# Three bf16 passes in place of f32 products: the scores and relative terms of the last of four layers

## The chip, the cores and the metric

The kernel runs on 1 core of one Trainium2 chip. The metric is the device time of one execution in microseconds (us). Several executions are timed; one more is taken with the hardware profiler, and everything read from a trace belongs to that one.

The engines are TensorE (PE; its weight loads are shown apart as PEld), VectorE (DVE), ScalarE (ACT), GpSimd (POOL) and SyncE (SP). SP issues nearly all DMA transfers here.

## The reference, cut to what matters

The network takes x of 4 sequences by 1024 tokens by 128 features through four layers. Each layer normalizes x, computes an attention-like branch `s` and a feed-forward branch `g`, and adds `s * silu(ffn)`. The change touches the fourth layer, a causal attention of 16 heads of 8 features with a relative term:

```
xn  = layernorm(x)
q, k, v = split_heads(xn @ Wq.T), split_heads(xn @ Wk.T), split_heads(xn @ Wv.T)     # (b, 16, n, 8)
ex  = rel_embed[ns].reshape(n, 16, 8).transpose(1, 0, 2)                             # 256 embeddings
srel = srel_skew(einsum('bhnd,hmd->bhnm', q, ex))      # row n shifted so that column = distance
qk  = (einsum('bhnd,bhmd->bhnm', q, k) + srel) / sqrt(8)
att = softmax(qk - 1e9 * triu(1, k=1))                 # causal
s   = einsum('bhnm,bhmd->bhnd', att, v) @ Wp.T + bp
g   = silu(gated feed-forward of xn, hidden size 384)
out = x + s * g
```

All inputs and outputs are float32, except the integer weights of this layer's feed-forward.

## The kernel before, in words

Layers 0 to 2 come first and hold x in SBUF (`x_all`). Layer 2 writes x to DRAM (`x3`). Then `load3` and `prepare3` load and turn the weights of the last layer, and `layer3` does the rest. An instruction stream for each engine is recorded while the Python code runs; the engines follow their streams in order and meet through semaphores. The order on one engine is close to that of the code, but a scheduler moves some instructions.

**The embeddings.** `prepare3` spreads the 256 embeddings with POOL copies into a zeroed tile `pad` (L1653), turns it on PE and has `W["emb"]`: 8 features of one head on partitions 32j to 32j+7, for j = 0 to 3, and 256 distances in columns. The column of distance 0 is subtracted from the others (L1660, L1661). Distances beyond 255 need no relative term then.

**A batch begins.** `begin3` loads one sequence of x, normalizes it, turns it (`xnT`), multiplies by `WqT` and `WkT` in two halves of 512 tokens (L1835), copies the products by ACT into `qk` (L1836), and stores them in DRAM (L1837). Values go the same way (`v`, `vd`). For the first sequence all of it runs at once, before the loop. For the others it is a generator (`beside`) that the loop moves on by one step a unit, from the fourth unit of the third group of the sequence before.

**Groups, units and tiles.** A group is 4 heads of one sequence; there are 16. `project3` loads the group's q and k from DRAM into `q` and `kk`, head j on partitions 32j to 32j+7. A group has 8 units, one for each block of 128 queries, in the order `ORDER3 = (7, 0, 6, 1, 5, 2, 4, 3)`, so that long and short rows take turns. A unit with t+1 blocks of keys has one tile of up to 512 columns, or two where t is over 3: 192 tiles in all.

**The relative term.** `relative3` multiplies 128 queries by the 256 embeddings, for two heads and two blocks at a time (L1914, in row slots 32j of PE's array), copies the result by ACT into `r` (L1916) and stores it in DRAM as `flat` with rows of 384 (L1919, L1920). `shear3` reads it back with a row step of 383 (L1935, L1937, L1941), which turns the column into the distance to the query, as the tile `rel`. POOL then sets what lies before or behind with affine selects (L1945). The tile of long units (`relb`) is in the pool `p2` with two buffers, that of short ones (`rels`) in `p1` with one. The loop calls `part(n + 7)` for `relative3` and `ahead(n + 3)` for `shear3`.

**Scores.** `scores3` multiplies q by k for 4 heads side by side (L1978, row slots 32j, one PSUM bank for each head, one set of 4 banks). DVE adds rel, scales, and keeps the running minimum `low` (L1993; L1986 for columns that need no rel). ACT takes the exponential and the row sums (L2000). DVE turns 32 by 32 blocks (L1737) and PE weighs the values (`weigh3`, L2014), in pieces that the loop puts between tiles. `vb` is the tile of values, filled by POOL (`values3`, L1899) when the last unit of the group before has been weighed; `drain(values)` stands in `weigh`.

**The loop.** It goes over the tiles:

```
next(fill, None)                      # DVE's comparison of this tile
transpose(...)                        # of an older tile, on DVE
step()                                # a piece of weighing, on PE
next(fill, None)                      # the score products of the next tile, on PE
```

At the last tile of a unit there follow the next group's `project3`, `part(n + 7)`, `values3`, a step of `beside`, and `ahead(n + 3)`.

`temp` is a pool of three buffers of 4 KB a partition, shared by x, the normalized x, `qk`, `v`, `r` and tiles of the feed-forward.

Of the kernel before, what the change touches and what calls it, by code (L numbers as in the profile page):

```python
# [19 lines left out]
P = 128  # L20
# [9 lines left out]
def _constants():  # L30
# [7 lines left out]

    parts.append(("ident", np.eye(P)))
    parts.append(("tri", row <= col))  # L40
# [5 lines left out]

    parts.append(("sel3", (row // 32 == col // 8 % 4) & (row // 8 % 4 == col // 32)))
    parts.append(("of_a", (row // 8 % 4) == np.arange(4)[None, :]))
    parts.append(("of_t", (row % 8) == np.arange(8)[None, :]))
# [43 lines left out]
class Kit:  # L93


    def __init__(self, tc, const, const_sb):
        self.tc, self.nc = tc, tc.nc
        self.const_sb = const_sb
# [6 lines left out]
    def c(self, name):  # L105
        at, n = CONST_AT[name]
        return self.const_sb[:, at : at + n]
# [1511 lines left out]
def spread(a):  # L1619

    return a.rearrange("p (i j r) -> p i j r", j=4, r=32)[:, :, :, 0:8]
# [6 lines left out]
def prepare3(k, w, W, ps):  # L1628
# [18 lines left out]
    W["emb"] = new("emb", [P, 4, 256])  # L1647
    with k.tc.tile_pool(name="pad3", bufs=1) as rp:
        pad = rp.tile([P, 2, 512], F32, tag="pad", name="pad")
        nc.vector.memset(pad, 0.0)  # L1650
        for c in range(2):
            for i in range(4):
                nc.gpsimd.tensor_copy(spread(pad[:, c, :])[:, i], heads_of(W["rel"][:, c, :])[:, i])  # L1653
        for i in range(4):
            k.transpose_tiles(ps, "tr", [pad[:, c, i * P : (i + 1) * P] for c in (0, 1)], W["emb"][:, i, :])

        e0 = rp.tile([P, 4], F32, tag="e0", name="e0")
        nc.vector.tensor_copy(e0, W["emb"][:, :, 0])
        for i in range(4):
            nc.vector.tensor_scalar(W["emb"][:, i, :], W["emb"][:, i, :], e0[:, i : i + 1], None, op0=ALU.subtract)  # L1660
        nc.vector.tensor_scalar(W["emb"][:, :, 0], e0, -1.0, None, op0=ALU.mult)  # L1661
# [10 lines left out]
def layer3(k, W, x3, out, eps5, ps):  # L1672
# [12 lines left out]
    with ExitStack() as st:  # L1685
# [16 lines left out]
        def ahead(n):  # L1702
            if n < len(units):
                t = units[n][2]
                rels[n] = shear3(k, p2 if t > 3 else p1, flats[n // 8, t // 2], t)
# [5 lines left out]
        batch[0] = {}  # L1711
# [9 lines left out]
        weights, transposes, weighs, out_of = {}, [], [], {}  # L1721
# [19 lines left out]
        def weigh(n):  # L1741
            nonlocal values
            b, i, t = units[n]
            at, pair = n // 8, t // 2
            if n % 8 == 2:
                out_of[at] = ps.tile([P, 8, 32], F32, tag="o", name="po")
            o = out_of[at]
            yield from weigh3(k, weights.pop((at, pair)), vb, o, pair)
            if n % 8 == 7:
                drain(values)  # L1750
# [18 lines left out]
        for x, (n, first) in enumerate(tiles + [(len(units), 0)] * 4):  # L1769
# [16 lines left out]
            if pos == 3 and i == 2 and b + 1 < NB:  # L1786
                batch[b + 1] = {}
# [7 lines left out]
            if pos == 6 and at + 1 < 4 * NB:  # L1795
                values = values3(k, p1, batch[(at + 1) // 4], vb, (at + 1) % 4)
                next(values)
            next(beside, None)
            ahead(n + 3)
# [13 lines left out]
def begin3(k, W, p1, p2, temp, ps, dram, x3, b, eps5, seq):  # L1813
# [4 lines left out]
    k.layernorm(p2, x.rearrange("p h a d -> p (h a) d"), xn, eps5)  # L1818
# [10 lines left out]
    seq["qk"] = dram.tile([2, P, T], F32, tag="qk", name="qk")  # L1829
    for n, name in enumerate(("WqT", "WkT")):  # L1830
# [314 lines left out]
```

## Time and profile before

| | |
|---|---|
| median of 3 runs | 3271.13 us (3264.41 to 3277.84) |
| the profiled execution's own time | 3261.59 us |
| its span, first to last instruction | 3259.9 us |
| mean granted TensorE clock in it | 0.734 |
| DVE's first comparison of the last layer | 2208.69 us from the span's start |
| busy from there to 3238.4 us: PE, DVE, ACT, POOL | 865, 807, 626, 290 of 1029.7 us |

Lines such as L1978 are lines of the kernel before. In a group of instructions, `out<-in` names the tiles; then come partitions x elements, the count, busy time in us and the mean duration of one in ns, and after the second bar the time that the engine had been idle just before, with what ended it. In a row of windows, the first number after the bounds is the length, then the busy time of each engine with the count of instructions, then the granted share of the TensorE clock, the busy share of the 16 DMA engines and GB/s. In a timeline the columns are start, duration and engine. A wait line has the waiting group, what it waited for, us in total, times, and the longest.

### The profile page before, as it was taken

Reading aid. Unit: us, or ns where it says so; the run is one execution under the profiler, and the core shown is the slowest. Engines: PE = TensorE matmul, PEld = TensorE weight load, DVE = VectorE, ACT = ScalarE, POOL = GpSimd, SP = SyncE. Lnnn points to the kernel's source line nnn. Section 1 sums busy time; section 2 is a strip of 40 time slices with the busy share of each in tenths; the row PEclk is TensorE's granted clock in tenths of the full one; section 3 lists DMA queues with packets and bytes.
Section 4 is the critical chain, followed back from the end, with each engine's and each line's share of the span. In section 5 each row is a group of like instructions: output and inputs, shape, how many; then the busy total and the mean of one; then the engine's idle time right before and its main releaser. Section 6 shows DMA issues by size and latency. Waiting matters only on the chain. (4 is left out here: it accounts for less than half of the span.)

```text
span 3259.9 us, 50636 instructions
## 1 busy us (share of the span) xinstructions
PE 2317.2 (71%) x18321; PEld 1327.2 (41%) x18321; DVE 2307.1 (71%) x5534; ACT 1487.5 (46%) x3248; POOL 1174.5 (36%) x1104
## 2 busy tenths in 40 slices
PE   5787777677776777965533772557888888888885
PEld 2555555222322323651101222344545555555553
DVE  5555545878878886657868878437678778777786
ACT  4555453433333334344322561125665665755663
POOL 3344334144444444224577222332322322323322
PEclk9888888678788888985555666566766766756676
DMA  3000000100000000320433444347677677766772
GB/s 89 3 1 1 1 1 1 35 0 0 0 0 1 0 0 33 105 84 0 111 95 105 109 108 99 110 119 209 187 213 207 181 209 217 202 195 193 200 231 71
DMA packets 396446, 303.46 MB, mean 93 GB/s; under 512 B 96272, under 2 KB 380812, under 8 KB 390564
## 3 DMA queue, kind: packets, MB, share of 16 engines
q1 hardware_dynamic: 395044, 296.03, 32.2%
q10 hardware_dynamic: 1152, 4.19, 0.4%
q8 instruction: 144, 2.36, 0.3%
q14 instruction: 106, 0.87, 0.1%
HBM read 160.63 MB, written 138.94 MB: 92 GB/s over the span
## 5 line engine op out<-in xcount | busy, mean ns | idle before, releaser
L2000 ACT ACTIVATE neg<-neg,low 128x640 f32<-128x640 f32 (+7 forms) x512 | 390.0, 763 | 153.9 <-DVE low L1993 153.8
L1945 POOL TENSOR_SCALAR_AFFINE_SELECT rel<-rel 128x512 f32<-128x512 f32 x288 | 179.9, 637 | 565.6 <-DMA rel<-flat 357.3
L1737 DVE STREAM_TRANSPOSE wT<-neg 128x640 f32<-128x640 f32 (+7 forms) x512 | 362.0, 753 | 7.6 <-ACT neg L2000 6.9
L1978 PE MATMUL score<-k,q 8*128 8x512 f32 (+3 forms) x1536 | 295.0, 747 | 91.2 <-DVE low L1993 91.0
L1993 DVE CUSTOM_DVE_ANT_0 neg<-score,rel,low 128x128 f32<-128x128 f32 (+3 forms) x448 | 217.5, 516 | 152.5 <-PE score L1978 105.6
L1914 PE MATMUL pr<-emb,q 8*128 8x256 f32 x1024 | 245.2, 569 | 45.0 <-ACT r L1916 27.2
L2014 PEld LDWEIGHTS po<-wT,vb 128*32 128x32 f32 x10240 | 208.1, 140 | 143.3 <-issue 78.0
L2014 PE MATMUL po<-wT,vb 128*32 128x64 f32 (+1 forms) x10240 | 242.9, 259 | 31.7 <-issue 17.3
L1914 PEld LDWEIGHTS pr<-emb,q 8*128 8x128 f32 x1024 | 153.6, 269 | 124.4 <-ACT r L1916 62.9
L1916 ACT COPY r<-pr 128x512 f32<-128x512 f32 x256 | 138.4, 581 | 144.2 <-PE pr L1914 95.1
L1993 DVE CUSTOM_DVE_ANT_0 neg<-score,rel 128x512 f32<-128x512 f32 (+3 forms) x320 | 149.3, 520 | 26.7 <-issue 15.4
L1978 PEld LDWEIGHTS score<-k,q 8*128 8x128 f32 x1536 | 103.0, 249 | 153.9 <-DVE low L1993 127.8
L835 PE MATMUL pg<-xnT,w 128*128 128x512 f32 x256 | 148.4, 663 | 7.7 <-DVE h L839 4.5
L214 PE MATMUL pt<-ident,three 128*24 128x128 bf16 x64 | 9.2, 295 | 201.9 <-DVE three L211 201.9
L788 POOL TENSOR_TENSOR prod<-rest,kv 128x2048 f32<-128x2048 f32 x32 | 145.6, 4599 | 18.4 <-ACT rest L778 18.4
L837 PE MATMUL pu<-xin,w 128*128 128x512 f32 x256 | 140.5, 632 | 14.3 <-DVE h L839 7.9
L826 PE MATMUL po<-h,w 128*128 128x512 f32 x256 | 129.6, 627 | 27.1 <-DVE h L839 27.1
L838 ACT ACTIVATE h<-pg 128x512 f32<-128x512 f32 x128 | 75.9, 595 | 156.2 <-PE pg L835 152.7
L1986 DVE TENSOR_SCALAR_CACHE_REDUCE neg<-score 128x384 f32<-128x384 f32 (+2 forms) x192 | 79.7, 415 | 69.3 <-PE score L1978 69.3
L1050 PE MATMUL ph<-xin,upT 128*128 128x512 bf16 (+1 forms) x128 | 71.3, 588 | 78.5 <-DVE xin L1044 77.7
L1455 PE MATMUL read<-kt,const_sb 128*128 128x128 f32 x256 | 50.1, 366 | 94.2 <-POOL kt L1450 94.2
L431 PE MATMUL px<-hT,xbcT 128*128 128x512 f32 x256 | 115.4, 595 | 0.0
(621 smaller groups left out, 5690.5 us busy)
## 6 DMA issues: line engine op xcount, KB each, us to landing
flat<-r SPq DMA_DIRECT2D x256, 256.0 KB
rel<-flat SPq DMA_DIRECT2D x112, 512.0 KB
flat<-r SPq DMA_DIRECT2D x256, 128.0 KB
rel<-flat SPq DMA_DIRECT2D x96, 256.0 KB
kt<-kd SPq DMA_DIRECT2D x16, 512.0 KB
qt<-qd SPq DMA_DIRECT2D x16, 512.0 KB
kdc<-kdd SPq DMA_DIRECT2D x16, 512.0 KB
ktc<-ktd SPq DMA_DIRECT2D x16, 512.0 KB
```

What stands on the lines that cost most here:

```text
L788: nc.gpsimd.tensor_tensor(prod, attn.rearrange("p (t h g) -> p t h g", t=4, g=16)[:, t].unsqueeze(2).to_broadcast(each), kv[:, t, 1, :].re ...
L826: nc.tensor.matmul(po, W["w2"][:, e, c, :], h[:, c, :], start=(e == 0 and c == 0), stop=(e == 7 and c == 1))
L835: nc.tensor.matmul(pg, W["w1"][:, e, c * P : (c + 1) * P], xnT, start=True, stop=True)
L837: nc.tensor.matmul(pu, W["w3"][:, e, c * P : (c + 1) * P], xin, start=True, stop=True)
L1737: nc.vector.transpose(weights[at, pair][j][:, t % 2, 0 : (t + 1) * P], S[j][:, 0 : (t + 1) * P])
L1914: nc.tensor.matmul(to[:, m, :], q[at, t * P : (t + 1) * P], W["emb"][at, i, :], start=True, stop=True)
L1916: nc.scalar.copy(r[:, n], to)
L1945: nc.gpsimd.affine_select(out=rel[:, :, slot(back), :], in_=rel[:, :, slot(0), :], compare_op=op, fill=fill, base=0, pattern=[[0, 4], [-si ...
L1978: nc.tensor.matmul(sc[:, j, 0 : last - first], q[at(j), 1 + t * P : 1 + n], kk[at(j), first:last], start=True, stop=True)
L1993: nc.vector.tensor_tensor_reduce(out=neg[:, begin:last], in0=sc[:, j, begin - first : last - first], in1=rel[:, j, slot : slot + (last - b ...
L2000: nc.scalar.activation(neg[:, 0:n], neg[:, 0:n], AF.Exp, bias=here, scale=-1.0, accum_out=group["sums"][:, j, t : t + 1])
L2014: nc.tensor.matmul(o[32 * j : 32 * j + 32, 2 * pair + m.start : 2 * pair + 2, :], vb[:, kb, j].rearrange("p a d -> p (a d)"), weights[j][: ...
```

## The change

The last layer's q, k and embeddings are split into three bf16 parts whose sum is the float32 value: the upper 16 bits, the upper 16 bits of what is left, and the rest. In `begin3`, ACT copies each half of the product to `rest`; POOL copies the upper half-words of `rest` (a bf16 view of it) to `three`, subtracts, and does so again. For each half, q goes to DRAM once with its three parts and k three times, so that 24 rows (8 features by 3 parts of q) meet 24 rows that all hold one part of k. The scores then take three accumulating bf16 matmuls (parts of k), and so do the relative terms (parts of the embeddings). The slots keep their places, 32j, with 24 rows instead of 8. The two q tiles are allocated once and hold two zero columns ahead. `prepare3` copies the embeddings three times into `pad` and splits them with three ACT copies and two DVE subtractions.

All rel tiles come from `p2`. `ahead(n + 3)` and the filling of `vb` now stand ahead of the step of `beside`, and the filling after `ahead`. The constants are loaded in two parts, of which the larger lies in memory that is freed before the last layer. The layernorm's small tiles of `begin3` lie in `p1`.

```diff
 def spread(a):
-    return a.rearrange("p (i j r) -> p i j r", j=4, r=32)[:, :, :, 0:8]
+    return a.rearrange("p (i j r) -> p i j r", j=4, r=32)[:, :, :, 0:24].rearrange("p i j (d a) -> p i j d a", a=3)
...
-                nc.gpsimd.tensor_copy(spread(pad[:, c, :])[:, i], heads_of(W["rel"][:, c, :])[:, i])
+                for a in range(3):
+                    nc.gpsimd.tensor_copy(spread(pad[:, c, :])[:, i, :, :, a], heads_of(W["rel"][:, c, :])[:, i])
...
+        for third in range(3):
+            nc.scalar.copy(W["emb"][:, third], emb)
+            if third < 2:
+                nc.vector.tensor_tensor(emb, emb, W["emb"][:, third], ALU.subtract)
...
-                rels[n] = shear3(k, p2 if t > 3 else p1, flats[n // 8, t // 2], t)
+                rels[n] = shear3(k, p2, flats[n // 8, t // 2], t)
...
             if n % 8 == 7:
-                drain(values)
+                ripe.append(values)
...
+            ahead(n + 3)
+            fill_values()
             next(beside, None)
-            ahead(n + 3)
...
-    seq["qk"] = dram.tile([2, P, T], F32, tag="qk", name="qk")
-    for n, name in enumerate(("WqT", "WkT")):
-        qk = temp.tile([P, T], F32, tag="temp", name="qk")
+    seq["q"] = dram.tile([P, 3, T], BF16, tag="qd", name="qd")
+    seq["k"] = dram.tile([P, 3, 3, T], BF16, tag="kd", name="kd")
+    for name in ("WqT", "WkT"):
         for half in range(2):
             tok = slice(half * 512, (half + 1) * 512)
             pp = ps.tile([P, 512], F32, tag="tr", name="pp")
             nc.tensor.matmul(pp, W[name], xnT[:, tok], start=True, stop=True)
-            nc.scalar.copy(qk[:, tok], pp)
-        nc.sync.dma_start(out=seq["qk"][n], in_=qk)
-        yield
+            three = temp.tile([P, 3, 512], BF16, tag="temp", name="three")
+            rest = temp.tile([P, 512], F32, tag="temp", name="rest")
+            nc.scalar.copy(rest, pp)
+            upper = rest.bitcast(BF16).rearrange("p (t two) -> p t two", two=2)[:, :, 1]
+            for third in range(2):
+                nc.gpsimd.tensor_copy(three[:, third], upper)
+                nc.gpsimd.tensor_tensor(three[:, 2] if third else rest, rest, three[:, third], ALU.subtract)
+            if name == "WqT":
+                nc.sync.dma_start(out=seq["q"][:, :, tok], in_=three)
+            else:
+                for a in range(3):
+                    nc.sync.dma_start(out=seq["k"][:, a, :, tok], in_=three)
+            yield
...
-            at, t = slice(32 * j, 32 * j + 8), 2 * pair + m
-            nc.tensor.matmul(to[:, m, :], q[at, t * P : (t + 1) * P], W["emb"][at, i, :], start=True, stop=True)
+        for third in range(3):
+            for j, to in zip(js, pr):
+                at = slice(32 * j, 32 * j + 24)
+                nc.tensor.matmul(
+                    to[:, m, :], q[at, first : first + P], W["emb"][at, third, i, :], start=(third == 0), stop=(third == 2)
+                )
...
-        for j in range(4):
-            nc.tensor.matmul(
-                sc[:, j, 0 : last - first], q[at(j), 1 + t * P : 1 + n], kk[at(j), first:last], start=True, stop=True
-            )
+        for third in range(3):
+            for j in range(4):
+                nc.tensor.matmul(
+                    sc[:, j, 0 : last - first], q[at(j), 2 + t * P : 2 + n], kk[at(j), third, first:last],
+                    start=(third == 0), stop=(third == 2),
+                )
```

`project3` loads, for each of the four heads, 24 rows of 1024 for q and 24 rows of 3 x 1024 for k, by as many transfers as before. The rest of the diff moves constants.

## The prediction

> **What bounds the kernel now.** First the page: its totals and the row of the granted clock, because the change touches TensorE (PE), GpSimd (POOL) and the DMA queue of SyncE (SP) at once. All edits but one split load lie in the last layer, which starts at 2150 us; the fourth fence cuts it into opening, loop and tail.
>
> ```profile
> span 3259.9 us, 50636 instructions
> PE 2317.2 (71%) x18321; PEld 1327.2 (41%) x18321; DVE 2307.1 (71%) x5534; ACT 1487.5 (46%) x3248; POOL 1174.5 (36%) x1104
> PEclk9888888678788888985555666566766766756676
> ```
>
> Then the groups, for the lines that change:
>
> ```profile
> L1945 POOL TENSOR_SCALAR_AFFINE_SELECT rel<-rel 128x512 f32<-128x512 f32 x288 | 179.9, 637 | 565.6 <-DMA rel<-flat 357.3
> L1978 PE MATMUL score<-k,q 8*128 8x512 f32 (+3 forms) x1536 | 295.0, 747 | 91.2 <-DVE low L1993 91.0
> L1914 PE MATMUL pr<-emb,q 8*128 8x256 f32 x1024 | 245.2, 569 | 45.0 <-ACT r L1916 27.2
> ```
>
> Each f32 matmul stands there as two instructions; scores and relative terms hold 540 us of PE. What that is worth is read from the waits of VectorE (DVE) in the loop (columns: us in total, times, longest):
>
> ```profile
> DVE neg L1993 <- PE score L1978: 105.7, 53, 9.7
> DVE neg L1986 <- PE score L1978: 44.1, 14, 7.3
> ```
>
> ```profile
> 2150.00:2208.70 58.70, 36.30 (x145) 25.29 (x143) 14.01 (x54) 19.86 (x39) 16.50 (x24) 0.65 0.62 174
> 2208.70:3238.40 1029.70, 864.99 (x13166) 544.15 (x13167) 806.94 (x2551) 625.71 (x1474) 289.75 (x414) 0.68 0.68 196
> 3238.40:3259.90 21.50, 9.47 (x140) 5.02 (x140) 2.61 (x6) 0.37 (x1) 4.68 (x2) 0.79 0.09 25
> ```
>
> Columns are length, then busy PE, weight loads, DVE, ACT, POOL, then clock, DMA share and GB/s. In the loop DVE idles 1029.7 - 806.9 = 223 us. I went through the timeline for all 192 groups of scores. In 81 of them DVE stands idle for over 0.3 us (192 us in all) until the last score matmul ends. Between the end of DVE's comparison before and the end of the score those 81 hold 240 us of PE: 125 scores, 22 relative terms, 50 feed-forward, 22 weighting, the rest small, 13 idle. The other 111 groups have their scores ready: a faster PE gives nothing there. So 540 us of faster matmuls cannot return more than these stalls, and a stall shrinks by no more than its own length.
>
> **Three passes for f32.** Two widths of a score group at half clock:
>
> ```profile
> 2653.13 0.81 PE L1978 MATMUL score<-k,q 8*128 8x128 f32 x8
> 2655.34 2.09 PE L1978 MATMUL score<-k,q 8*128 8x512 f32 x8
> ```
>
> (2.09 - 0.81)/384 is 3.33 ns a column and 0.38 us is fixed. No row has four bf16 matmuls beside one another on 32-row slots. Alone, a 24-row bf16 pass of 512 columns (pb, L222) takes 580 ns at the median, a 128-column one (L214) 314: 0.69 ns a column. A quarter of the f32 rate would be 0.83. So three passes of 512 cost 1.06 to 1.28 us plus 0.38, which is 0.69 to 0.79 of 2.09; the weight loads, 98 ns in bf16 (L222) against 281 in f32, shorten the fixed part. I take 0.74 for both kinds. Relative slices begin at an odd column of q, for which no row exists; a bf16 load twice as long would still be shorter than today's. In the 81 stalls, each capped by its length: -37 us (bounds -30 and -43).
>
> **The clock.** The clock records change only at steps of 3.41 us. I sorted the loop's steps by PE time of anything but scores and relative terms: with none, the next step had the full clock in 0 of 84; with 1 to 1.5 us in 24%; with 2 to 3 us in 79%; over 3 us in all 32. In 77 steps of the span the 8-row matmuls were over 90% of PE's work and over 2 us long: the next was at half clock in all 77. The windows say it too; the first is full of 8-row matmuls, the second of weighting (128 rows):
>
> ```profile
> 2192.00:2196.00 4.00, 4.00 (x21) 2.83 (x16) 0.57 (x2) 2.22 (x4) 0.00 (x0) 0.50 1.11 369
> 2240.00:2244.00 4.00, 3.50 (x185) 2.97 (x178) 2.26 (x13) 0.04 (x1) 1.28 (x2) 0.93 1.11 357
> ```
>
> So occupied rows seem to count, and 24 rows are three times 8. With pass lengths at 3/4, work by rows times columns of these two lines rises by 2.25. Recounting each step so, with the limit that parts full from half today (0.35 of the array's full work in a step), full steps go from 36% to 42%, or 0.68 to 0.71 in the mean: 5% faster, another -9 us in the 81 stalls. Below, 24 rows count as little as 8 (0 us). Above, everything runs at full clock: scores and relative terms at 0.50 of today, the rest at 0.65, which leaves -91 us of the stalls in place of -46.
>
> The Trainium skill (TensorE: Matmul & The Clock Gate, Part 1) says that the clock is set by how busy PE has recently been, and that idleness lowers it. The first window above, fully busy at 0.50, does not agree if busy means time. By that rule this change, which leaves PE idler, would cool the clock, and the sum would go towards the fourth rival's.
>
> **Distances with two buffers.** SP's queue waits 226.9 us for DVE's `low` ahead of rel loads (L1935), since the small rel tile has one buffer; flat stores, project and value loads stand behind it. With two, that wait goes; ACT's r (146.7 us at L1919) is late next. DVE waited for rel only at the start, so the worth is bounded by the 13 us in which PE idled inside stalls: 0 to -13, I take -8. The value copies now stand behind the selects on POOL. They are needed two units later, so 0; uncovered, 4 x 1.03 us (L1899) would hold weighting, and the scores behind it in PE's order, in each of 15 groups.
>
> **What the thirds cost at the opening.** Up to the first comparison at 2208.69 nothing covers them.
>
> ```profile
> 2176.84 2.06 SPq L1837 DMA_DIRECT2D qk<-qk  x2
> 2183.57 3.06 SPq L1895 DMA_DIRECT2D vr<-vd  x4
> 2186.90 0.62 SPq L1919 DMA_DIRECT2D flat<-r  x1
> ```
>
> The embeddings first: 24 pad copies instead of 8 (16 x 0.207 = 3.3 us), then two rounds of a 1024-wide ACT copy (1.06, from L778) and a DVE subtraction (1.24, from L2050's 0.69 for 512), 4.6 us. In the order of instructions both subtractions stand before the layernorm, which began at 2165.8 as DVE came free: +7 (5 to 8). Then q and k: per half two POOL copies (0.52, half of L1899's 1024) and two subtractions (1.06, L1127), 3.2 us; four halves from 2175.5 end at 2188.3. SP now stands in the order 2 q stores, 6 k stores, v, 4 q loads, 4 k loads, 4 v loads, then flats. The six stores and v's issue add 2 us after the last half, the k loads wait some 3 us for 1.2 MB at the 300 to 430 GB/s seen then, and 8 issues take 4.4 us: first flat at 2198 to 2199 instead of 2186.9, +12. Dearest rows (0.30 per 128 columns, L1646; 1.92, L1359) make four halves 25 us: +24. Cheapest: +8. From the first flat to the first comparison are 28 stores of 0.55 us on SP, as before. Opening: +19 (13 to 32).
>
> At three batch changes the same POOL work (12.8 us) and 6 more SP issues lie beside 60 us of loop per group. But q's second half is made on the last unit of a group, and the first relative matmuls on it stand three tiles (3 x 1030/192 = 16 us) later in PE's order. ACT's copy 0.6, POOL 3.2, a unit's selects before it 1.9, store 2.8 (2176.84 to 2179.63 above) and load 3.5 are 12 us. I take +5 in sum for the three. Nothing there can gain. Above, each stops PE as long as the longest select waited for rel in the loop (13.8 us, DMA): +41. Traffic grows by 4.2 MB a batch, 16.8 MB in all, 58 us at the loop's 196/0.68 GB/s, in engines that are 68% busy over 1030 us: off the path.
>
> **Sum.** -37 - 9 - 8 + 19 + 5 = -30 us. The profiled execution took 3261.59 us, its span 3259.9; it becomes 3232. The median of the three runs is 9.5 us above it, so I forecast 3241.
>
> **Rivals.**
> 1. The clock wakes: 24 rows count fully. Scores become ready early, DVE and exponentials rule. -91 - 8 + 24 = -75: 3196. For it: 128-row windows at 0.93. Against: bf16 chains of layer 2 ran at 0.5. 18%.
> 2. The stalls change owner: passes give -37 alone, nothing else, against 24: -13, 3258, no measurable change (0.5% is 16 us, about what a measurement of this kernel can tell from none). For it: 50 of 240 us are feed-forward. 21%.
> 3. Slower: q's chain through POOL stops PE at each batch change. 41 there and 28 at the opening, against -37: +32, 3303. It decides from stops of (37 + 9 + 8 - 19)/3, about 12 us each. For it: POOL's selects wait up to 13.8 us for DMA, and the thirds stand behind them. Against: 16 us of slack. 18%.
> 4. The clock sinks to 0.5: 1.36 times all, passes at 1.02: the stalls grow by 33, +57 with the costs, 3328. Against: the 77 steps, in which this work already counts for nothing. 5%.
>
> **Numbers.** My forecast has 38%. Faster by over 0.5% (under 3255): 38 + 18 = 56%; within: 21%; slower: 18 + 5 = 23%. From 3185, just under rival 1, to 3300, just short of rival 3, leaves out about two in ten.
>
> **What would show it.** Score groups of 12 bf16 instructions near 1.55 us at half clock; DVE's waits for scores some 100 instead of 150 us in the loop; clock 0.70 to 0.73 there; first comparison near 2228; SP's wait for `low` gone. I am wrong if the loop's DVE idle time stays near 223 us, if relative matmuls wait for q's DMA by more than 10 us at batch changes, or if the loop's clock leaves 0.66 to 0.76.

## The result, and the profile after

The changed kernel takes 3292.72 us (median; 3284.12 to 3301.32), the kernel before 3262.98 us beside it (eight runs each; the three ahead of the prediction had a median of 3271.13): a ratio of 1.0092, 95% interval 1.0073 to 1.0112. It is slower by some 30 us where 30 us less was forecast. The profiled execution took 3290.7 us, 29 us more than that of before. A ratio is made against the kernel before on the same chip; below, differences between kernels are differences of ratios times 3263 us.

The page after, totals and granted clock:

```profile
span 3288.8 us, 53223 instructions
PE 2189.1 (67%) x19599; PEld 1246.2 (38%) x19601; DVE 2300.4 (70%) x5536; ACT 1488.3 (45%) x3251; POOL 1231.0 (37%) x1170
PEclk9898888688778878975556675656766767777677
```

TensorE lost 128 us of work and the span grew. The groups that answer to those of before (busy us, mean ns, then the idle time before them):

```profile
L1982 POOL TENSOR_SCALAR_AFFINE_SELECT rel<-rel 128x512 f32<-128x512 f32 x288 | 180.3, 637 | 463.3 <-DMA rel<-flat 382.2
L2016 PE MATMUL score<-k,q 24*128 24x512 bf16 (+3 forms) x2304 | 201.8, 431 | 155.1 <-DVE low L2032 150.9
L1949 PE MATMUL pr<-emb,q 24*128 24x256 bf16 x1536 | 196.1, 358 | 77.8 <-ACT r L1953 41.5
```

Scores and relative terms together fell from 540 to 398 us. But idle time before relative matmuls rose from 45.0 to 77.8 us. The last layer again in opening, loop and tail (columns as before):

```profile
2150.00:2233.00 83.00, 33.64 (x175) 20.31 (x175) 15.77 (x56) 22.62 (x42) 32.08 (x52) 0.58 0.55 154
2233.00:3267.70 1034.70, 739.05 (x14407) 467.28 (x14407) 796.51 (x2551) 624.27 (x1474) 329.45 (x448) 0.70 0.76 209
3267.70:3288.80 21.10, 9.30 (x141) 4.97 (x140) 2.57 (x6) 0.37 (x1) 4.68 (x2) 0.80 0.13 26
```

The opening is 24 us longer. The loop has 126 us less PE work, a clock of 0.70 as forecast, and is 5 us longer: DVE idles 238 instead of 223 us in it. The DMA engines go from 68% to 76% busy. What DVE waits for in the loop (us, times, longest):

```profile
DVE neg L2032 <- issue: 113.4, 52, 9.7
DVE neg L2032 <- POOL rel L1982: 85.6, 10, 18.8
...
DVE neg L2032 <- DMA rel<-flat: 11.7, 6, 3.3
DVE neg L2032 <- PE score L2016: 8.3, 10, 3.3
...
DVE neg L2025 <- PE score L2016: 5.1, 4, 2.1
```

In the kernel before, "issue" and the selects stood at:

```profile
DVE neg L1993 <- issue: 42.5, 18, 6.8
DVE neg L1993 <- POOL rel L1945: 13.9, 1, 13.9
```

By this view scores, 150 us before, are nearly gone, POOL's selects stand at 85.6 (13.9 before), and "issue" at 113.4 (42.5), a wait for which the view names nobody. A view that names one releaser per wait misleads here, so I took the score and select times from the trace, group by group: in nearly every stall, before and after, the tile's first comparison starts less than 0.25 us after the last score product ends. Idle time in which the score products ended last is 220 us in 94 groups (215 in 100 before; the prediction, which counted more narrowly, had 192 in 81), and only 13 us are left to selects. In the stalls, from the end of DVE's comparison before to the end of the score products, PE spent:

| us | score | relative | weighing | feed-forward | rest | PE idle | all |
|---|---|---|---|---|---|---|---|
| before | 143 | 27 | 23 | 52 | 12 | 15 | 273 |
| after | 84 | 32 | 18 | 55 | 20 | 49 | 258 |

So the faster passes gave 59 us there, and PE's own waiting took 34 back. Of its 49 us, 21 end at a relative matmul (0.4 before), 12 at a weighing, 7 at a feed-forward product. The stretches are 15 us shorter in sum, but DVE idles for 233 of the 258 us, where it idled for 215 of 273: it has less other work in them.

### The profile page after: what moved, and what is told of

Read it like the earlier page. It is cut to its first block, busy times and chain, and to the rows that moved or that the text cites. A ratio compares the mean times of both kernels' runs of the same rounds, so it can differ in the third digit from the quotient of the medians.

```text
span 3288.8 us, 53223 instructions
## 1 busy us (share of the span) xinstructions
PE 2189.1 (67%) x19599; PEld 1246.2 (38%) x19601; DVE 2300.4 (70%) x5536; ACT 1488.3 (45%) x3251; POOL 1231.0 (37%) x1170
## 5 line engine op out<-in xcount | busy, mean ns | idle before, releaser
L2016 PE MATMUL score<-k,q 24*128 24x512 bf16 (+3 forms) x2304 | 201.8, 431 | 155.1 <-DVE low L2032 150.9
L2053 PE MATMUL po<-wT,vb 128*32 128x64 f32 (+1 forms) x10240 | 231.0, 245 | 58.7 <-issue 37.1
L1949 PE MATMUL pr<-emb,q 24*128 24x256 bf16 x1536 | 196.1, 358 | 77.8 <-ACT r L1953 41.5
L2053 PEld LDWEIGHTS po<-wT,vb 128*32 128x32 f32 x10240 | 193.0, 130 | 139.4 <-issue 69.8
L1949 PEld LDWEIGHTS <-q 24*128 24x128 bf16 x1536 | 114.1, 118 | 152.7 <-issue 91.3
L2016 PEld LDWEIGHTS <-q 24*128 24x128 bf16 x2304 | 71.7, 107 | 227.3 <-issue 182.6
L1457 PE MATMUL read<-kt,last_sb 128*128 128x128 f32 x256 | 49.4, 363 | 94.3 <-POOL kt L1452 94.3
```

The source lines that it names most:

```text
L1949: nc.tensor.matmul(to[:, m, :], q[at, first : first + P], W["emb"][at, third, i, :], start=(third == 0), stop=(third == 2))
L2016: nc.tensor.matmul(sc[:, j, 0 : last - first], q[at(j), 2 + t * P : 2 + n], kk[at(j), third, first:last], start=(third == 0), stop=(third ...
L2053: nc.tensor.matmul(o[32 * j : 32 * j + 32, 2 * pair + m.start : 2 * pair + 2, :], vb[:, kb, j].rearrange("p a d -> p (a d)"), weights[j][: ...
```

## The experiments

All medians and ratios in one table; each kernel is told of below it. The last column is the ratio times 3263 us. A quotient of the two medians can differ from the ratio on record by a few us; it does most in e5, where it gives -15 instead of -21.

| | us | ratio to before, 95% | to before, us |
|---|---|---|---|
| e1 moved steps, f32 | 3283.5 | 1.0054 (1.0035 to 1.0072) | +18 |
| e8 second buffer only, f32 | 3274.3 | 1.0039 (1.0022 to 1.0056) | +13 |
| e2 thirds, old order | 3290.1 | 1.0076 (1.0054 to 1.0097) | +25 |
| e7 next sequence's step first | 3279.5 | 1.0058 (1.0035 to 1.0081) | +19 |
| e3 no thirds on GpSimd | 3263.5 | 0.9994 (0.9983 to 1.0006) | -2 |
| e4 k stored once | 3282.4 | 1.0046 (1.0026 to 1.0065) | +15 |
| e6 narrow second and third pass | 3300.8 | 1.0109 (1.0075 to 1.0143) | +36 |
| e5 one part of k loaded | 3245.9 | 0.9936 (0.9915 to 0.9956) | -21 |
| e9 the same and 393 KB for nobody | 3269.1 | 1.0031 (1.0014 to 1.0047) | +10 |
| e13 e2 with one part of k | 3243.5 | 0.9934 (0.9913 to 0.9955) | -22 |
| e14 f32 and 393 KB for nobody | 3297.8 | 1.0102 (1.0081 to 1.0123) | +33 |
| e10 k loads on ACT's queue | 3280.8 | 1.0072 (1.0046 to 1.0097) | +23 |
| e11 e10, k once, DVE at the opening | 3273.9 | 1.0054 (1.0036 to 1.0072) | +18 |
| e12 e11, q loads on ACT's queue too | 3290.2 | 1.0086 (1.0057 to 1.0116) | +28 |
| e15 old order, k once, k loads spread | 3275.1 | 1.0029 (1.0013 to 1.0046) | +9 |
| e16 e7, k once, DVE at the opening | 3274.7 | 1.0039 (1.0022 to 1.0055) | +13 |
| e17 e15 with six of nine products | 3354.9 | 1.0272 (1.0249 to 1.0296) | +89 |
| e18 e16 with six of nine products | 3284.3 | 1.0060 (1.0039 to 1.0080) | +20 |

**The moved steps and the second buffer.** e1 is the kernel before with all of the change except the thirds.

```diff
-                rels[n] = shear3(k, p2 if t > 3 else p1, flats[n // 8, t // 2], t)
+                rels[n] = shear3(k, p2, flats[n // 8, t // 2], t)
-                drain(values)
+                ripe.append(values)
+            ahead(n + 3)
+            fill_values()
             next(beside, None)
-            ahead(n + 3)
```

> The kernel before with only the moved steps, the second buffer for the small rel tiles and the split constants; products stay f32. Theory A (the loss comes from the thirds of q and k at the opening and at the three batch changes): this kernel has none of them, so it lies at 0 to -13 us from the kernel before, ratio 0.996 to 1.000. Rival B (the loss comes from the moved steps: selects that wait for a load now stand ahead of the feed-forward's products and of the value copies in POOL's queue): it holds most of the loss, +15 to +30 us, ratio 1.005 to 1.009.

e2 is the changed kernel with those lines as they were before.

> The changed kernel with its moved steps undone: small rel tiles with one buffer, ahead(n + 3) after the step of beside, values filled where the last weighing of a group ends. The thirds and the three passes stay. Theory A: the loss stays, 3285 to 3300 us against 3263 of the kernel before (ratio 1.007 to 1.012). Rival B: the passes' gain shows, -37 - 9 + 24 for the opening, so 3235 to 3260 (ratio 0.992 to 0.999).

e8 has only the first pair of those lines, in the kernel before (with the constants in two parts and the layernorm's small tiles in `p1`, which the memory needs).

> The kernel before with the second buffer for the small rel tiles alone (and the split constants): f32 products, old order of the steps. By the prediction's term -8, with 0 to -13 as its bounds: 3253 to 3266 (ratio 0.996 to 1.000). Rival (SP, freed of its wait for low, issues flats and rel loads earlier and these collide with others; the loss of the moved steps comes from the buffer): slower, 3272 to 3284 (ratio 1.002 to 1.006).

e7 is the changed kernel with the step of the next sequence first.

```diff
+            next(beside, None)
             ahead(n + 3)
             fill_values()
-            next(beside, None)
```

> The changed kernel with the step of beside ahead of ahead(n + 3) again, as before; the fill of the values stays where the change puts it, and the small rel tiles keep two buffers. Theory B2 (the selects that stand between the feed-forward's products on GpSimd cost the loop): 8 to 20 us less than the changed kernel, 3273 to 3285 (ratio 1.002 to 1.006). Rival (the scheduler orders GpSimd's queue by what is ready, so that the place in the code does little when rel loads are late): 3288 to 3297 (ratio 1.007 to 1.010).

In f32 the moved steps cost 18 us, and 13 of them come with the second buffer alone; by the forecast it saved 8. No run has the split constants and the layernorm's tiles by themselves; e8's first comparison with rel comes at 2207.75 us, so nothing is lost ahead of the loop. What can be seen in the loop is that the scheduler puts selects between the products `h` of the feed-forward. POOL in e8, first feed-forward step of the second sequence (start, us, engine):

```profile
2533.93 0.73 POOL L1874 TENSOR_TENSOR h<-h,up 128x256 f32<-128x256 f32 x1 [4.96 <-DMA rel<-flat]
2535.45 1.22 POOL L1952 TENSOR_SCALAR_AFFINE_SELECT rel<-rel 128x512 f32<-128x512 f32 x2 [0.79 <-DMA rel<-flat]
2536.63 0.72 POOL L1874 TENSOR_TENSOR h<-h,up 128x256 f32<-128x256 f32 x1
2537.31 0.63 POOL L1952 TENSOR_SCALAR_AFFINE_SELECT rel<-rel 128x512 f32<-128x512 f32 x1
2537.91 0.73 POOL L1874 TENSOR_TENSOR h<-h,up 128x256 f32<-128x256 f32 x1
```

PE of e8 beside it:

```profile
2537.41 0.49 PE L1878 MATMUL po<-downT,h 128*128 128x128 f32 x2 [1.03 <-POOL h L1874]
2538.70 2.08 PE L1878 MATMUL po<-downT,h 128*128 128x128 f32 x8 [0.80 <-POOL h L1874]
```

And POOL of the kernel before at the same step:

```profile
2536.12 2.10 POOL L1867 TENSOR_TENSOR h<-h,up 128x256 f32<-128x256 f32 x3 [2.19 <-ACT up L1866]
2538.16 1.94 POOL L1945 TENSOR_SCALAR_AFFINE_SELECT rel<-rel 128x512 f32<-128x512 f32 x3
```

Before, three products run in one go and the selects after them. In e8 the first product starts when ACT's `up` is done, at 2533.85 (the view puts this wait down to rel). The second could start at 2534.40 by its `up`, but starts 2.2 us later, behind two selects, which waited 0.79 us for their rel transfer; the third stands behind one more select. PE's `po` waits for the products, with the scores behind it. Over the 16 feed-forward steps 13 selects stand among the products in e1 and e8, 1 before, 18 after; DVE's idle time in the feed-forward groups (1, 5, 9, 13) is 97 us in e8 and 86 before. That is 11 of the 22 us that DVE idles longer in the loop of e8's trace; where the rest comes from is open. The count of such selects is no price by itself: the changed kernel has 18 and idles 89 us in these groups, e12 below has none and idles 106. With the thirds, taking the moved steps and the buffer out (e2) gains only 5 us, within the intervals. Their cost does not add to that of the rest. The order in e7 gains 11 us (here the intervals just overlap).

**What the thirds cost on GpSimd.** In e3, ACT writes the bf16 product three times and POOL does nothing, so scores are those of rounded values.

```diff
-            nc.scalar.copy(rest, pp)
...
-                nc.gpsimd.tensor_copy(three[:, third], upper)
-                nc.gpsimd.tensor_tensor(three[:, 2] if third else rest, rest, three[:, third], ALU.subtract)
+            nc.scalar.copy(three, pp.unsqueeze(1).to_broadcast([P, 3, 512]))
```

> The changed kernel without the work of GpSimd on q and k: ACT writes the bf16 product three times into `three`, and the rest is left out, so that q and k are wrong in value but all transfers and all passes stay. Theory A: the opening is 10 to 13 us shorter, and the first groups of the second to fourth batch give back their 27 us: 3250 to 3262 us (ratio 0.996 to 1.000). Rival B: only the opening is shorter: 3278 to 3283 (ratio 1.005 to 1.006).

It gains 32 us on the change: 11 in the opening, where the first comparison with rel comes at 2222.3 instead of 2233.0, and 18 between the first and last comparison. Of those, 16 lie in the groups in which the next sequence begins (3, 7, 11: DVE idle 35.6 instead of 51.3 us). The groups after them (4, 8, 12) keep 46 us, against 25.5 before, so POOL's thirds are not what makes those slow. The opening shows the work, four of these pairs for q, four for k (changed kernel, start, us):

```profile
2181.31 0.61 POOL L1860 COPY three<-rest 128x512 bf16<-128x512 bf16 x1 [6.12 <-ACT rest L1856]
2182.00 1.16 POOL L1861 TENSOR_TENSOR rest<-rest,three 128x512 f32<-128x512 f32 x1
...
2195.98 1.15 POOL L1861 TENSOR_TENSOR three<-rest,three 128x512 bf16<-128x512 f32 x1
```

```profile
2193.34 5.42 SPq L1866 DMA_DIRECT2D kd<-three  x6
...
2209.28 0.80 SPq L1956 DMA_DIRECT2D flat<-r  x1
```

Four halves take 15.8 us, not 12.8, and the first flat leaves 22.4 us later than before, where 7 and 12 were forecast.

In e4, k goes to DRAM once, and the load reads each row three times; the bytes of the load are the same.

```diff
-                for a in range(3):
-                    nc.sync.dma_start(out=seq["k"][:, a, :, tok], in_=three)
+                nc.sync.dma_start(out=seq["k"][:, :, tok], in_=three)
...
+            in_=bass.AP(src.tensor, src.offset, [(3 * T, 8), (0, 3), (1, 3 * T)]),
```

> The changed kernel with k stored once with its three parts, and each row read three times by the load (a step of 0 in DRAM), which takes 4 of 6 k stores and two thirds of their bytes away and changes no other instruction. Theory A: SP's six issues of 0.53 us are two, the opening is 2 to 5 us shorter and each batch change 1 to 3 us: 3280 to 3288 us (ratio 1.005 to 1.008). Rival C (the added traffic slows rel loads and the loading of code): 3265 to 3278 (ratio 1.001 to 1.005).

Fifteen us less, with POOL's order the same: 6.3 MB of stores are not free either.

**TensorE.** e6 narrows the second and third pass to 32 columns, so their products are left out.

```diff
+            wide = 32 if third else last - first
-                    sc[:, j, 0 : last - first], ..., kk[at(j), third, first:last],
+                    sc[:, j, 0:wide], ..., kk[at(j), third, first : first + wide],
```

> The changed kernel, in which the second and the third pass of scores and relative terms cover only 32 columns (the rest of their products is left out); the number of instructions and all transfers stay. Theory D (TensorE's matmuls no longer bound the loop; what is left of DVE's stalls are chains through ACT, GpSimd, SP and code loading): at most 12 us from the changed kernel, 3281 to 3293 (ratio 1.005 to 1.009). Rival (the passes still bound the stalls, as the prediction had it): 25 to 40 us from it, 3253 to 3268 (ratio 0.997 to 1.001).

Less PE work, no gain. In the plain groups (0, 2, 6, 10, 14, 15) DVE idles less, 30 instead of 52 us, and in the groups in which a sequence begins (3, 7, 11) it idles more, 78.5 instead of 51.3. The scheduler's order changed too, and with less work on PE the loop's granted clock fell to 0.66, which slows all other products, so e6 doesn't settle how much of the loop PE's speed still sets.

**The load of k.** e5 loads one of k's three parts, and all three passes read it (196 KB a group instead of 590).

```diff
-    kk = p2.tile([P, 3, T], BF16, tag="k", name="k")
+    kk = p2.tile([P, T], BF16, tag="k", name="k")
-                in_=seq["k"][head].rearrange("d a b t -> (d a) b t"))
+                in_=seq["k"][head, :, 0, :].rearrange("d a t -> (d a) t"))
```

> The changed kernel, in which project3 loads only the first of k's three parts (a third of the bytes: 196 KB instead of 590 KB a group) and all three passes read it; the values of the scores are therefore off by what the two other parts hold. TensorE's work and its number of instructions stay. Theory C (the load of k delays what stands behind it in the DMA engines: rel loads, and the loading of TensorE's code, for which TensorE waits 57 us in the loop instead of 20): those waits fall to 25 to 40 us, and the groups that begin a sequence get 5 to 9 us shorter: 3268 to 3282 us (ratio 1.001 to 1.005). Rival (the loads are hidden): 3288 to 3297 (ratio 1.007 to 1.010).

e9 is e5 with the 393 KB loaded again, into a tile that nobody reads.

```diff
+    more = p2.tile([P, 2, T], BF16, tag="more", name="more")
+    nc.sync.dma_start(out=more[0:96], in_=seq["k"][32 * i : 32 * i + 32, :, 1:3, :].rearrange("d a b t -> (d a) b t"))
```

> The kernel that loads one part of k (scores off by the two other parts), plus one transfer a group of the two other parts, 393 KB, behind it in SP's queue into a tile that nobody reads. GpSimd's order of instructions stays nearly that of the kernel with one part (97.5% of its sequence in common; the changed kernel has 69% in common with it), the bytes are those of the changed kernel. Theory O (the 47 us lie in the order: with k's large load the scheduler puts selects among the feed-forward's products, 18 instead of 6, and the value copies ahead of selects): 3246 to 3265 us (ratio 0.994 to 1.001). Rival C (the bytes: TensorE waits for its code and rel loads land later while k comes in): 3278 to 3297 (ratio 1.005 to 1.010).

e13 is e2 (old order, one small rel buffer) with e5's edit.

> The kernel with the thirds in the old order of steps and one buffer for the small rel tiles, with one part of k loaded (scores off by the two other parts). Against the kernel with the old order and all of k (3290 us). Theory K (the load of k carries the loss, by its bytes and by the order that it makes the scheduler choose, whatever the written order of the steps): 30 to 50 us less, 3240 to 3262 (ratio 0.994 to 1.000). Rival M (the moved steps and the buffer decide, and one part of k helps only together with them): 3270 to 3290 (ratio 1.003 to 1.008).

e14 is the kernel before, constants in two parts, with a load of 393 KB for nobody behind k's.

```diff
+            more = p2.tile([P, T], F32, tag="more", name="more")
+            nc.sync.dma_start(out=more[0:96], in_=bass.AP(src.tensor, src.offset, [(0, 3), (T, 32), (1, T)]))
```

> The kernel before, f32 and in its own order, with the split constants and one more transfer of 393 KB a group behind the loads of k, into a tile that nobody reads. No thirds, no passes, no moved step. Theory K: 15 to 30 us slower than the kernel before (ratio 1.005 to 1.009), with nine selects among the feed-forward's products on GpSimd instead of one. Rival (traffic of that size is hidden, as the prediction priced it): 0 to 6 us (ratio 1.000 to 1.002).

Here the sign turns. Without the 393 KB a group the change is worth 51 us more, with the old order 46 us (44 and 42 by the medians), and both kernels beat the one before. The loop of e13 and three of DVE's waits in it:

```profile
2233.00:3217.90 984.90, 721.02 (x14405) 456.20 (x14404) 796.80 (x2543) 622.89 (x1474) 327.82 (x446) 0.71 0.76 213
```

```profile
DVE neg L2031 <- issue: 58.3, 24, 10.5
DVE neg L2031 <- PE score L2015: 49.0, 32, 8.8
DVE neg L2031 <- POOL rel L1981: 32.9, 14, 6.6
```

PE's waiting inside the stalls is 33 us there, of which 1.0 ends at a relative matmul (21 in the changed kernel). The same bytes given back cost 31 us in e9 (23 by the medians), where 95% of POOL's instructions in the last layer stand in e5's order, and 33 us in the f32 kernel of e14 (36 by the medians). But e14 is not the bytes alone: of POOL's instructions 95% keep the order of before, and yet 9 selects stand among the feed-forward's products where there was 1; 9 us come ahead of the first comparison with rel (2217.95), and 18 of the 29 us that DVE idles longer in the loop lie in the groups 4, 8 and 12, where e9, with the same bytes, idles 29 us against 26 in e5. So e9 is the nearer measure of the bytes.

The other 20 us between e9 and the change come without a byte: there 89% of POOL's order is common. In the traces DVE idles 46 us in the groups 4, 8 and 12 of the change and 29 in e9's; no score product waits for k's transfer in either. That the scheduler takes three parts in one transfer to be ready later would explain it; I did not test that. Against a simple price for the order speak e10 and e12 below, which have 9 and no selects among the products and no measurable gain on the change. In e14 what grew is the wait of POOL's selects for rel and DVE's for the selects (13.9 before); the first line is of the kernel before:

```profile
POOL rel L1945 <- DMA rel<-flat: 341.8, 72, 13.8
POOL rel L1956 <- DMA rel<-flat: 405.7, 76, 20.9
...
DVE neg L2004 <- POOL rel L1956: 41.0, 4, 21.8
```

Counted by the semaphore updates, of which the traces lack 2 to 6%, a rel transfer takes about 4.3 us from issue to landing at the median before and 4.9 after, but 4.9 in e5 as well, so the median does not show the load; in e14 the slowest tenth goes from 5.6 to 8.9 us. The 16 extra loads are 6.3 MB, at the 209/0.76 = 275 GB/s of the loop's windows 23 us of the engines' full rate: in engines that were 68% busy the load cost its own length or somewhat more. The mean load does not tell the kernels apart: e13's loop, the fastest, has the same 0.76 as the changed kernel.

**Can the load be hidden?** These keep all nine products of parts. e10: `nc.scalar.dma_start` for k's loads.

> The changed kernel, exact, with the four loads of k a group issued by ACT in place of SP. The scheduler's order on GpSimd becomes like that of the kernel with one part (9 selects among the feed-forward's products instead of 18, four units selected ahead of the value copies of three groups instead of three or two). Theory O: 3250 to 3272 us (ratio 0.996 to 1.003), less some us for ACT's 64 issues. Rival C: the bytes stay, 3282 to 3297 (ratio 1.006 to 1.010).

e11: e10, with e4's edit, and at the opening DVE takes the thirds of the second halves (`eng = nc.vector if b == 0 and half else nc.gpsimd`).

> The kernel before this one in the list, with k stored once and its rows read three times by the load, and at the first sequence the second half of q and of k split by DVE instead of GpSimd. Both theories: the opening gets 3 us shorter by the stores and 4 to 7 us by DVE, first comparison with rel near 2223 instead of 2233 us, and 5 to 10 us come from the stores at the batch changes: 12 to 20 us under the kernel before it.

e12: e11 with q's loads on ACT's queue too.

> The same with the loads of q on ACT's queue too. No select is left among the feed-forward's products in GpSimd's order (0 instead of 12 in the kernel before this one, 18 in the changed kernel). Theory O: the groups with the feed-forward get 2 to 4 us shorter each, 8 to 15 us under the kernel before this one. Rival: ACT, which takes the loads in order, waits for the q stores at three batch changes and holds exponentials and copies of r behind them: 5 to 25 us over it.

e15: e2's order, e4's and DVE's edits, and k's load by one head a unit over four units:

```diff
-            if pos == 2:
+            if 2 <= pos <= 5:
```

> An exact version made of what the runs show: thirds and three passes, old order of steps and one small rel buffer, k stored once, its four loads issued one a unit (positions 2 to 5 of a group) instead of at once, and the second half of q and k at the first sequence split by DVE. Theory K: k comes in smaller portions (147 KB at a time), 5 selects among the products instead of 20: 3250 to 3270 us (ratio 0.997 to 1.003). Rival M: 3275 to 3290 (ratio 1.004 to 1.009).

e16: e7 with e4's and DVE's edits.

> The other exact version: the changed kernel with the step of beside first, k stored once, and DVE for half of the first sequence's thirds. If the gains of these three edits add (13, 10 and 4 us): 3263 to 3270 us (ratio 1.000 to 1.003). If the bytes of k's stores and the order share one cause: 3272 to 3282 (ratio 1.003 to 1.007).

Another queue for k can't be told from the change (1.0072 beside 1.0092, the intervals overlap), and q on it as well seems to lose 10 us (here too they overlap). The Trainium skill (DMA: Bandwidth & Descriptors, Issuing engines are not separate DMA queues) says that transfers issued by different engines run on the same 16 DMA engines, so that only issue time is saved; e10, in which nothing measurable is gained, agrees. Against the change, e15 and e16 bring 21 and 17 us, most of it what e4 brought alone, and none of the five beats the kernel before. DVE at the opening was to bring the first comparison forward and left it at 2233.7 in e11 (2230.9 in e16, 2226.9 in e15); why, I did not settle.

**Fewer bytes in more transfers.** e17 (on e15) and e18 (on e16) leave out the three smallest of the nine products: the passes use 24, 16 and 8 rows, k's load is 393 KB, in 12 transfers a group instead of 4.

```diff
-                    sc[:, j, 0 : last - first], q[at(j), 2 + t * P : 2 + n], kk[at(j), third, first:last],
+                    sc[:, j, 0 : last - first], q[rows, 2 + t * P : 2 + n], kk[rows, third, first:last],
...
+        for a in range(3):
+            nc.sync.dma_start(out=kk[32 * j + 8 * a : 32 * j + 8 * a + 8, 0 : 3 - a], in_=src[:, 0 : 3 - a])
```

with `rows = slice(32 * j, 32 * j + 24 - 8 * third)`.

> The kernel with the old order of steps, one small rel buffer, k stored once and its loads spread over four units, and in it six of the nine products of parts: the first pass uses 24 rows, the second 16, the third 8, so that the three smallest products (middle by low, low by middle, low by low) are left out and a group's k load shrinks from 590 to 393 KB. SP issues 12 small k transfers a group instead of 4. If the bytes of the load carry the cost (47 us for 393 KB, so half of it for 197 KB): about -23 us against the run that had all nine products, a ratio of 0.994 to 0.998 to the kernel before. If 48 busy rows in place of 72 let the clock fall from 0.70 to the 0.68 of before, a third of the passes' gain goes and it stays at 1.000 to 1.004. If the number of transfers counts and not their bytes, it is slower than the run with nine products, above 1.004.

> The same six of nine products (the three smallest are left out) in the kernel whose steps stand ahead of the value copies as in the change, with the step of the next sequence first, k stored once, loads not spread. If the bytes carry the cost in both orders alike: about -23 us against the run with nine products, 0.994 to 0.999 to the kernel before, and within 0.003 of the spread version. If the order that the scheduler chooses carries half of the cost, the two versions may differ by up to 24 us (0.007).

Both lost against the runs with nine products, e18 7 us (the intervals overlap) and e17 79 us, although 3.1 MB less moved. One stretch of the loop in e16 and then in e18:

```profile
2235.00:3255.00 1020.00, 742.60 (x14528) 470.35 (x14520) 793.93 (x2540) 624.27 (x1475) 325.94 (x443) 0.71 0.74 206
```

```profile
2235.00:3255.00 1020.00, 752.50 (x14203) 473.27 (x14206) 788.48 (x2519) 618.86 (x1463) 326.38 (x443) 0.68 0.72 202
```

The clock fell from 0.71 to 0.68 with fewer rows occupied (0.70 to 0.68 from e15 to e17), and in e18 SP issues 12 transfers of k in some 6 us where 4 took some 3 in e16. So fewer bytes did not make these kernels faster; whether the clock, the number of transfers or the order took it back is not shown. Which part made e17 so slow stays open; its order differs as well (the q stores wait for POOL's thirds up to 14.5 us, where e15 has 4.1).

## Why the prediction was wrong, step by step

- **Three passes.** Right for the scores, whose groups of 512 columns at half clock take 0.70 of the time before (factor taken: 0.74); the relative terms' busy time went to 0.80 (245 to 196 us). The way to 0.74 was partly off. The 128-column row (L214) is a transposition with 128 rows and 24 columns, no 24-row pass, and the 580 ns of L222 mix both clocks. By the two lines below a column costs (1.47 - 0.51)/384 = 2.5 ns for three passes, 0.83 each, which was the upper bound; it is the fixed part that fell, from 0.38 to 0.19 us.

```profile
2659.72 1.47 PE L2016 MATMUL score<-k,q 24*128 24x512 bf16 x12 [2.28 <-DVE low L2032]
2665.69 0.51 PE L2016 MATMUL score<-k,q 24*128 24x128 bf16 x12 [1.02 <-DVE low L2032]
```

- **The clock.** Right: 0.70, and 0.71 in e13, for the 0.71 of the recount. e17 and e18 show the other direction. Such averages are weak evidence (kernels with all nine products range from 0.69 to 0.71), but the steps of 3.41 us are not: in the changed kernel's last layer all 41 steps that 24-row passes filled to over 90% of PE's work, for over 2 us, were followed by half clock. What these steps count is in the last section.
- **The step that failed** is the end of the opening's part: "Traffic grows by 4.2 MB a batch, 16.8 MB in all, 58 us at the loop's 196/0.68 GB/s, in engines that are 68% busy over 1030 us: off the path". The sum has no term for it. Of that traffic, the 6.3 MB that e5 and e13 take away were worth 51 and 46 us, and the 6.3 MB of stores in e4 15 us. Of the load's price about 31 us (23 by the medians) came back in e9 with the bytes alone, in nearly the same order; the rest goes with what the scheduler made of the one large transfer, and which transfers the bytes hold up was not taken apart. One sign of it: in the first five units of the groups 4, 8 and 12, which follow the start of a sequence, the last select ended 11 to 16 us before its comparison, and now 1.4 to 5. A mean of 68% did not show how little the chain r to flat to rel has to spare there.
- **Without that load the rest holds as a sum.** The forecast without the buffer's term is -37 - 9 + 5 = -41 us for the loop and -22 with the opening; e13, which has neither the load's extra parts nor the second buffer, runs from the first to the last comparison with rel in 984.3 us against 1027.2, -43, and is 22 us faster by its ratio. The single terms are not shown by that: e13 still carries the stores (15 us in e4) and POOL's thirds (18 us of the loop in e3, 5 forecast), so the passes must have given more than was forecast, or these costs overlap. The close agreement is in part luck.
- **Two buffers.** Forecast -8, measured +13 alone (e8). SP's wait did shrink, from 226.9 to 106.9 us, and ACT's r is late next as said; but the bound "below 0" was wrong. The forecast looked at the wait alone and not at what the scheduler does with a freed buffer; selects between the feed-forward's products are half of e8's added idle time at most.
- **The opening.** +19 forecast, +24 measured. The layernorm began 5.8 us later (7 taken). From there to the first flat the thirds' chain took 17 instead of 12, POOL 3 us dearer, the stores and loads behind it more; 2 us more passed between the first flat and the first comparison.
- **Batch changes.** +5 forecast. Taking POOL's work away (e3) gives 18 us back in the loop, some of it by another order. The groups after them lose 20 us (DVE idle 46 instead of 25.5), with or without POOL's work; with one part of k they have 26 (e5) and 22 (e13), so that loss goes with the load, but not with its bytes: with all bytes in two transfers they have 29 (e9). PE's relative matmuls waited 14.1 us in three waits for q's transfer, none over 6.5. In sum that is over the 10 us which the forecast named as a sign of being wrong, and well under the third rival's 12 us each.
- **The rivals.** The third had the sign and nearly the time (3303), by luck: its mechanism, the q chain, stops PE only by a third of its price. The second had half of the truth, stalls that change owner: score products still end last in 220 us of idle time, and in front of them PE itself now waits. The sign that the forecast named for its own failure, DVE idle near 223 us in the loop, is what came (238).

## What to carry to other kernels

Give added transfers a price, at least the time that they hold the engines, and look at the chain that shares those engines, not at their mean load; a replicated operand (here three times three) can cost what the faster matmuls bring. To test it, add the bytes to a kernel that is otherwise the same (e9 on e5), and check that the order on the engines stayed: in e14 it did not. And where a scheduler orders the streams by its own estimates, a second buffer or another transfer size moves instructions of other stages: compare the order on the engine that all stages share (here POOL) before the time is forecast.

## What the runs showed of the hardware

**The clock went by rows and columns in use, over time.** For each step of 3.41 us in the last layer, take every matmul's columns streamed (by the score groups of 512 and 128 columns at full clock (0.83 - 0.35)/384/3 us = 1.25/3 = 0.42 ns each for bf16 and (1.14 - 0.50)/384 us = 1.67 ns for f32) times the share of the array's rows and columns that it occupies. Steps above 0.35 of the full array were followed by full clock and the others by half clock in 99% of 323 steps of the kernel before, and with a limit of 0.36 in 99% of 332 of the changed kernel. With the best limit on PE's busy time alone 70% and 74% agree, where half clock in every step would give 64% and 61%.

**PE waited for its own instructions.** In the changed kernel's loop 32 gaps of PE end 1.2 to 1.8 us after a 16 KB packet of its instruction queue landed, 57.3 us in all, 17.0 of them while DVE was idle (19 gaps, 20.5 and 4.3 us before; 67 and 11 in e13). Some of them are chance: the equally long intervals just before and after, 0.6 to 1.2 and 1.8 to 2.4 us, hold 8 and 14 gaps, 11 and 13 us. As e13 has as many, these waits are not what made the change slow. One of them, PE of the changed kernel:

```profile
2780.26 1.86 PE L2053 MATMUL po<-wT,vb 128*32 128x64 f32 x130
2786.86 0.65 PE L2053 MATMUL po<-wT,vb 128*32 128x32 f32 x22 [4.74 <-issue]
```

The DMA engines from 2781.5 to 2787 in it, in 40 slices:

```profile
DMA  9959494969859995999699999999999999999999
```

The 16 KB fetch began at 2783.99 and took 1.48 us among k's parts and rel, with all engines busy. The Trainium skill (Runtime: NRT & Kernel Launch, Instruction fetch mechanics) says that the cost of crossing a 16 KiB boundary is mostly hidden. These gaps differ. The loop has 14,407 matmuls and as many weight loads where it had 13,166, each shorter. That PE therefore asks for instructions at a faster pace, and that the fetches are late because they meet the kernel's transfers, would fit; no run tests it.
